# A fused two-block kernel on one core: the values of two channel tiles by seven products instead of eight

## The chip, the cores and the metric

The kernel runs on one core of a Trainium2 chip. The metric is the device time of the whole program in microseconds (us), less is better. Engines are named as the profile names them: PE (TensorE; PEld its weight loads), DVE (VectorE), ACT (ScalarE), POOL (GpSimd) and SP (SyncE, which issues most DMAs).

## The reference, cut to what matters

Two blocks, each `x = x + s * g`, on 2 batches of 512 tokens and 512 features, all float32. The first block is an autocorrelation with a small mixture of experts, the second a state-space mixer (128 heads of 64 channels in 8 groups, states of 128, chunks of 128 tokens) with a gated feed-forward layer. The change lies in the mixer, after its input's norm `h`:

```python
proj = jnp.einsum('bsd,od->bso', h, in_proj_w)
gate = proj[..., :D_INNER]
hBC = proj[..., D_INNER:D_INNER + CONV_DIM]
...
hBC = jax.nn.silu(causal_conv(hBC, conv_w, conv_b))
hid = hBC[..., :D_INNER].reshape(b, s, H_M, P_M)
...
hid_dt = hid * dt[..., None]
...
Y_diag = jnp.einsum('bcijh,bcjhp->bcihp', M, hc)
...
states = jnp.einsum('bclhn,bhcl,bclhp->bchpn', Bh, decay_states, hc)
...
yg = y * jax.nn.silu(gate)
...
out = jnp.einsum('bsd,od->bso', y, out_proj_w)
```

The values `hid` are 8192 channels: a projection of 512 features per channel, a causal convolution of four taps, a SiLU. The gate is a projection of the same size without the convolution.

## The kernel before, in words

The first part (about 600 us) computes the first block, the mixer's norm and decays, and the feed-forward layer. The rest, some 1670 us, is the mixer. Its work is cut into 16 **units** (8 groups of 16 heads, each for 2 batches), a unit into 8 **tiles** of 128 channels (two heads) by 512 tokens, and `step(d)` handles two tiles at a time. So a unit has four steps, told apart by `t` = 0, 2, 4, 6, and there are 63 steps and a tail. Each step works on several pairs of tiles at different stages:

- tiles `a` (2d, 2d+1): `products` (L1170, L1179) multiply the decay matrices and the states into `py`, and `finish_y` (L1198, L1199) makes y on DVE.
- tiles `n` (the next pair): `transposed` (L1222, PE) and `values` (L1232, DVE) bring `hid` into token order; `decays` (ACT: clamp L1246, exp into PSUM L1260; DVE: multiplication L1261); `states` (PE L1268, ACT copy L1270, DVE L1274); `starts` (POOL L1286); and the gate's projection, `Gates`.
- tiles `h` (the pair after that): `channels` projects the values (L1140: four matmuls of 512 columns per tile) and `conv` takes the taps, the first on ACT (L1146), three on DVE (L1151). `silu` (L1502) ends them.
- tiles `p` (the pair before): POOL multiplies y by the gate (L1590), ACT squares it (L1211), POOL sums the squares (L1215).
- the unit before: `Output` multiplies it by the output weights, by seven products of 256 columns per pair of token rows (L1463), each added into `acc` on DVE (L1477): five, five and four in the steps t=2, 4, 6. Step t=0 has no output but projects B and C of the next unit (`inner`), and t=4 makes `inner_products` of them.

`Gates` makes the gate of a pair of tiles by Winograd's form of Strassen's scheme: the 256 weight columns and 512 tokens are halved, the 512 features too, and the 2x2 blocks are multiplied in seven products of two 256-column matmuls (L608) instead of eight. POOL forms sums of the weight blocks ahead (`row_sums`, L582); sums of `hT` are kept in `th` for all tiles. The partial sums that several blocks share are read out between the products, by ACT copies (L1335) and DVE adds (L1339), and the last product of a half accumulates in its PSUM bank.

The order of work is written out by hand: under `manual_schedule` each engine runs its instructions in program order, and waits are placed where tiles and PSUM banks are shared. The eight PSUM banks are `pj` 2, `tr` 2, `yy` 2, `of` 1, `de` 1. Of the 63 steps, 57 take the branch `if gates:`; the others (`plain` ones in the first and last unit) project the gate directly.

Of the kernel before, what the change touches and what calls it, by code (L numbers as in the profile page):

```python
# [15 lines left out]
P = 128  # L16
# [32 lines left out]
def fused_kernel(  # L49
# [41 lines left out]
    after = const.tile([P, P], F32, tag="after", name="after")  # L91
    make_lower_triangular(nc, after, val=1.0, diag=False)
    ones = const.tile([P, P], F32, tag="ones", name="ones")
    nc.gpsimd.memset(ones, 1.0)

# [27 lines left out]
    hand = early.enter_context(tc.tile_pool(name="hand", bufs=1, side="right"))  # L123
    epsum = early.enter_context(tc.tile_pool(name="eps", bufs=1, space=PSUM))
# [926 lines left out]
    with ExitStack() as sm:  # L1051
# [92 lines left out]
        def conv(ps, ct, dst):  # L1144

            nc.scalar.activation(  # L1146
                dst, ps, AF.Identity, bias=cb[:, ct : ct + 1], scale=cw[:, ct, KCONV - 1 : KCONV]
            )
            silus.append(dst)
# [69 lines left out]
        def transposed(s):  # L1219
            px = psum.tile([P, NCH, P], F32, tag="tr", name=f"px{s}", bufs=2)  # L1220
            for c in range(NCH):
                nc.tensor.transpose(px[:, c, :], hid[s][:, bass.ts(c, P)], ident)  # L1222
            return px
# [39 lines left out]
        def states(s, hcd):  # L1263

            u, g, b, t, h0 = place(s)
            pn = psum.tile([P, NCH - 1, P], F32, tag="tr", name=f"pn{s}", bufs=2)
            for c in range(NCH - 1):
                nc.tensor.matmul(pn[:, c, :], Bss[u][:, c, :], hcd[:, c, :], start=True, stop=True)  # L1268
# [24 lines left out]
        def gate(s, bank, room="sgt"):  # L1293

            u, g, b, t, h0 = place(s)
            pg = psum.tile([P, S], F32, tag=bank, name=f"gt{s}", bufs=1 + (bank == "pj"))
            project(lambda k: wgs[s // 2][:, k, bass.ts(s % 2, P)], b, pg)
            bufs = {} if room == "sgt" else {"bufs": 4}
            sgs[s] = wk.tile([P, S], F32, tag=room, name=f"sgt{s}", **bufs)
            return sgs[s], pg  # L1300

        class Gates:
# [4 lines left out]
            def __init__(self, s):  # L1307
# [3 lines left out]
                sw = wk.tile([P, 4, 2, P], F32, tag="sw", name=f"sw{s}", bufs=1)  # L1311
                sw = [sw[:, i] for i in range(4)]
                row_sums(w, *sw)
                self.factors = seven(w, sw, hT[:, :, bass.ts(b, S)], b)

            def multiply(self, *which):
                for i in which:
                    if i == 1:
                        self.ps = psum.tile(
                            [P, 2, HD], F32, tag="pj", name=f"gt{self.s}", bufs=2  # L1320
# [27 lines left out]
        def channels(s):  # L1348
# [3 lines left out]
            ps = psum.tile([P, S], F32, tag="pj", name=f"pjh{s}", bufs=2)  # L1352
# [19 lines left out]
        def inner_products(u):  # L1372

            pb = psum.tile([P, NCH, P], F32, tag="tr", name=f"pb{u}", bufs=2)
# [122 lines left out]
        outs, ahead, rest_of_sums = {}, {}, set()  # L1497
# [7 lines left out]
        def head():  # L1505
# [30 lines left out]
            pxs = [transposed(s) for s in range(2)]  # L1536
# [6 lines left out]
            for s, x in enumerate(hcd):  # L1543
# [11 lines left out]
        def step(d):  # L1555
# [43 lines left out]

            for s, py in zip(a[:1], pys):  # L1600
                finish_y(s, py)
            for s in n[:1]:
# [5 lines left out]
            for s in n[:1]:  # L1608
                decays(s, 1)
                starts(s)  # L1610
            first = [channels(s) for s in h[:1]]
            pxs = [transposed(s) for s in n]
# [12 lines left out]
            def squares():  # L1625
                if t == 0 and went:
                    pss = psum.tile([P, NCH], F32, tag="tr", name=f"ssq{u - 1}", bufs=2)
                    for c in range(NCH):
# [3 lines left out]
                            ones[:, 0:1],  # L1632
# [10 lines left out]
            if gates:  # L1643
                if o:
                    o.multiply(1)
                if projected is not None:
                    first.append(inner(projected, 0))
                for x in first[:1]:
                    conv(*x)
                for s in n[1:]:  # L1650
                    decays(s, 0)
                    decays(s, 1)
                    starts(s)
                hcd = [values(s, px) for s, px in zip(n[:1], pxs)]
                root()
                gates.multiply(1, 5)
                second = [channels(s) for s in h[1:]]
                gates.copy(0, 0)
                gates.multiply(2, 6)
                for x in first[1:]:  # L1660
                    conv(*x)
                hcd += [values(s, px) for s, px in zip(n[1:], pxs[1:])]
                if o:
                    o.add()
                    if t == 4:
                        o.sums(1)
# [32 lines left out]
                pss = squares()  # L1699
                gates.silu()  # L1700
                silu()
                mean(pss)
                if o:
                    o.add()
            else:
# [31 lines left out]
                for s, x in zip(n, hcd):  # L1737
# [20 lines left out]
            if n and not plain(d + 1) and d + 1 < steps - 1:  # L1758
# [150 lines left out]
```

## Time and profile before

| | us |
|---|---|
| median of three runs | 2275.12 (2275.07 to 2275.14) |
| profiled execution | 2273.2 |
| its span (first to last instruction) | 2271.5 |
| granted PE clock, mean | 0.998 |
| DVE busy, ACT busy, POOL busy | 1431.9, 1243.9, 1135.3 |
| L1140 pjh (values), PE busy | 467.5 in 1024 records, mean 599 ns |
| L608 gt from th and sw (three of the gate's products), PE busy | 175.6 in 684 records (57 steps, 12 each), mean 379 ns |

The profile counts each float32 matmul as two records (`x8` is one tile's four matmuls). The mean duration of a record includes the time in which its end overlaps the next one, so the pace of PE is read from the starts of successive groups. "Idle before" gives what an engine waited for; the last column of a group names who released it.

### The profile page before, as it was taken

Reading aid. Unit: us, or ns where it says so; the run is one execution under the profiler, and the core shown is the slowest. Engines: PE = TensorE matmul, PEld = TensorE weight load, DVE = VectorE, ACT = ScalarE, POOL = GpSimd, SP = SyncE. Lnnn points to the kernel's source line nnn. Section 1 sums busy time; section 2 is a strip of 40 time slices with the busy share of each in tenths; the row PEclk is TensorE's granted clock in tenths of the full one; section 3 lists DMA queues with packets and bytes.
Section 4 is the critical chain, followed back from the end, with each engine's and each line's share of the span. In section 5 each row is a group of like instructions: output and inputs, shape, how many; then the busy total and the mean of one; then the engine's idle time right before and its main releaser. Section 6 shows DMA issues by size and latency. Waiting matters only on the chain.

```text
span 2271.5 us, 33304 instructions
## 1 busy us (share of the span) xinstructions
PE 2239.9 (99%) x11776; PEld 1589.5 (70%) x11776; DVE 1431.9 (63%) x2761; ACT 1243.9 (55%) x2693; POOL 1135.3 (50%) x996
## 2 busy tenths in 40 slices
PE   8999999999999999999999999999999999999998
PEld 4545576864567777777777777777677777777776
DVE  5273578445776766666666666666767666766653
ACT  4141323315775657566666666666656565666650
POOL 4160532232454457444755474555556455645484
PEclk9999999999999999999999999999999999999999
DMA  4021366746553435444544444454545444544442
GB/s 169 1 93 37 127 218 217 257 167 214 155 165 121 130 121 163 137 139 152 164 123 130 158 126 124 136 177 132 150 129 163 121 130 121 177 130 139 148 140 93
DMA packets 195509, 323.37 MB, mean 142 GB/s; under 512 B 17680, under 2 KB 129168, under 8 KB 192912
## 3 DMA queue, kind: packets, MB, share of 16 engines
q1 hardware_dynamic: 188944, 300.28, 43.2%
q0 software_dynamic: 6400, 20.98, 2.4%
q8 instruction: 94, 1.54, 0.3%
q14 instruction: 71, 0.58, 0.1%
HBM read 294.45 MB, written 26.74 MB: 141 GB/s over the span
## 4 chain that ended last, share of the span: by engine, by line
PE 92%; ACT 3%; DVE 2%; DMA 1%; issue 1%; POOL 0%; SPq 0%; ACTq 0%; POOLq 0%; DVEq 0%
PE pjh L1140 18%; PE of L1463 14%; PE gt L608 13%; PE py L1170 5%; PE pjbc L1140 4%; PE pf L1019 4%; PE pn L1268 4%; PE py L1179 3%; PE ofy L1463 2%; PE sh L523 2%; PE hu L362 2%; PE pg L608 2%; PE pu L608 2%; PE gty L608 2%; PE px L1222 2%; PE gt L1140 2%
## 5 line engine op out<-in xcount | busy, mean ns | idle before, releaser
L1140 PE MATMUL pjh<-hT,wh 128*128 128x512 f32 x1024 | 467.5, 599 | 0.5
L1286 POOL TENSOR_TENSOR eb<-CT,eb 128x768 f32<-128x768 f32 x128 | 230.2, 1817 | 445.0 <-DMA eb<-ea_d 408.0
L1151 DVE SCALAR_TENSOR_TENSOR hid<-pjh,cw,hid 128x511 f32<-128x511 f32 (+2 forms) x384 | 286.8, 747 | 81.9 <-ACT hid L1146 72.9
L1140 PEld LDWEIGHTS pjh<-hT,wh 128*128 128x128 f32 x1024 | 187.8, 190 | 202.5 <-issue 200.2
L1246 ACT ACTIVATE cs<-cs,sl 128x128 f32<-128x128 f32 x1024 | 323.6, 388 | 1.0 <-DMA cs<-cs_d 1.0
L582 POOL TENSOR_TENSOR sw<-wg 128x256 f32<-128x256 f32 x114 | 83.9, 736 | 287.6 <-PE gt L608 287.6
L1261 DVE TENSOR_TENSOR cs<-de,CB 128x512 f32<-128x512 f32 x256 | 175.3, 685 | 78.3 <-ACT de L1260 78.3
L1146 ACT ACTIVATE hid<-pjh,cb,cw 128x512 f32<-128x512 f32 x128 | 99.2, 775 | 166.1 <-PE pjh L1140 166.1
L1260 ACT ACTIVATE de<-cs 128x512 f32<-128x512 f32 x256 | 154.1, 602 | 49.5 <-DVE cs L1261 43.3
L1170 PE MATMUL py<-cs,hc 128*64 128x128 f32 x2048 | 180.4, 276 | 0.0
L1477 DVE SCALAR_TENSOR_TENSOR acc<-of,rg,acc 128x256 f32<-128x256 f32 x192 | 92.1, 480 | 138.3 <-PE of L1463 137.6
L608 PE MATMUL gt<-th,sw 128*128 128x256 f32 x684 | 175.6, 379 | 0.0
L1590 POOL TENSOR_TENSOR y<-y,sgt 128x512 f32<-128x512 f32 x124 | 161.7, 1325 | 12.2 <-ACT sgt L1346 10.4
L1179 PE MATMUL py<-eb,st 128*64 128x128 f32 x1536 | 149.2, 273 | 0.0
L1215 POOL TENSOR_TENSOR sums<-sums,sq 128x512 f32<-128x512 f32 x110 | 139.9, 1272 | 18.4 <-ACT sq L1211 14.7
L1274 DVE SCALAR_TENSOR_TENSOR st<-st,sl,pn 128x64 f32<-128x64 f32 x512 | 103.8, 275 | 62.9 <-ACT st L1270 62.9
L608 PEld LDWEIGHTS gt<-th,sw 128*128 128x128 f32 x684 | 126.7, 190 | 21.4 <-issue 6.7
L1170 PEld LDWEIGHTS py<-cs,hc 128*64 128x64 f32 x2048 | 121.5, 137 | 15.4 <-issue 13.4
L1199 DVE SCALAR_TENSOR_TENSOR y<-hid,Dcol,y 128x512 f32<-128x512 f32 x128 | 126.8, 990 | 4.5
L1463 PE MATMUL of<-wt,y 128*128 128x256 f32 x512 | 120.6, 379 | 0.0
L1335 ACT COPY sgt<-gt 128x256 f32<-128x256 f32 x171 | 63.4, 371 | 104.4 <-PE gt L608 104.4
L1198 DVE TENSOR_TENSOR y<-py,el 128x512 f32<-128x512 f32 x128 | 87.5, 684 | 51.7 <-PE py L1179 51.7
(337 smaller groups left out, 4511.5 us busy)
## 6 DMA issues: line engine op xcount, KB each, us to landing
cs<-cs_d SPq DMA_DIRECT2D x128, 512.0 KB, 4.3
eb<-ea_d SPq DMA_DIRECT2D x256, 192.0 KB, 6.1
wh<-in_in_wT SPq DMA_DIRECT2D x64, 512.0 KB, 9.0
wg<-in_in_wT SPq DMA_DIRECT2D x64, 512.0 KB, 7.4
el<-ea_d SPq DMA_DIRECT2D x256, 128.0 KB, 7.6
wo<-wo_d SPq DMA_DIRECT2D x16, 1024.0 KB, 8.6
wop<-in_out_wT SPq DMA_DIRECT2D x39, 256.0 KB, 3.0
wo_d<-wop POOLq DMA_DIRECT2D x39, 256.0 KB, 2.8
```

Of the source, the lines that this page charges most:

```text
L608: nc.tensor.matmul(ps, x[:, k, :], y[:, k, :], start=(first and k == 0), stop=(k == 1), skip_group_check=True,)
L1140: nc.tensor.matmul(ps, w_of(k), hT[:, k, bass.ts(b, S)], start=(k == 0), stop=(k == KD - 1))
L1151: nc.vector.scalar_tensor_tensor(dst[:, j:], ps[:, : S - j], cw[:, ct, KCONV - 1 - j : KCONV - j], dst[:, j:], ALU.mult, ALU.add,)
L1170: nc.tensor.matmul(py[bass.ts(hh, HP), bass.ts(c, P)], hc[:, c, bass.ts(hh, HP)], M[:, hh, bass.ts(c, P)], start=True, stop=(c == 0),)
L1179: nc.tensor.matmul(py[bass.ts(hh, HP), bass.ts(c, P)], st[:, c - 1, bass.ts(hh, HP)], cte[:, hh, bass.ts(c - 1, P)], start=False, stop=True,)
L1215: nc.gpsimd.tensor_tensor(sums[u], sums[u], q, ALU.add)
L1246: nc.scalar.activation(m[:, bass.ts(c, P)], m[:, bass.ts(c, P)], AF.Relu, bias=sls[g][:, 3, b * NCH + c, h0 + hh : h0 + hh + 1], scale=-1.0,)
L1260: nc.scalar.activation(pe, m, AF.Exp, scale=-1.0)
L1261: nc.vector.tensor_tensor(m, pe, CBs[s // GT].rearrange("p c i -> p (c i)"), ALU.mult)
L1286: nc.gpsimd.tensor_tensor(eb_t[s], CTs[s // GT][:, P:].unsqueeze(1).to_broadcast([P, 2, S - P]), eb_t[s], ALU.mult,)
L1463: nc.tensor.matmul(ps, x[:, k, :], y[:, k, :], start=(first and k == 0), stop=(k == 3), skip_group_check=True,)
L1590: nc.gpsimd.tensor_tensor(y_of(s), y_of(s), sgs.pop(s), ALU.mult)
```

## The change

The values of a pair of tiles `h` are now made by the same seven-product scheme as the gate, by a new class `Values`; the 512-column products remain in the plain steps. Blocks of the result are completed inside their two PSUM banks (`pj`), so that `conv` reads them there: ACT copies a partial sum to the still unused `hid` tile, and DVE adds it back to the bank. The weight sums are made by POOL at the end of the step before, and of the four sums of each scheme one now overwrites a block of the weights in place.

The order of the step is rewritten for the 57 steps: transposition, values and decays of the first tile of `n` come first, its states are begun (`begun`) before the second tile's, both decays of a tile are separated by the copies of `Values`, both convs come in the second half of the step, and each output product has its addition right behind it. One `tr` bank becomes a third `pj` bank. `conv` is split so that C's DVE taps come last in step t=0. The `ones` and `after` matrices move to the early pool, and a column of ones is taken from `upper`.

```diff
@@ -1143,9 +1142,15 @@

         def conv(ps, ct, dst):

+            first_tap(ps, ct, dst)
+            taps(ps, ct, dst)
+
+        def first_tap(ps, ct, dst):
             nc.scalar.activation(
                 dst, ps, AF.Identity, bias=cb[:, ct : ct + 1], scale=cw[:, ct, KCONV - 1 : KCONV]
             )
+
+        def taps(ps, ct, dst):
             silus.append(dst)
             for j in range(1, KCONV):
                 nc.vector.scalar_tensor_tensor(
@@ -1216,8 +1221,9 @@

             return add

-        def transposed(s):
-            px = psum.tile([P, NCH, P], F32, tag="tr", name=f"px{s}", bufs=2)
+        def transposed(s, spare=False):
+            tag, bufs = ("pj", 3) if spare else ("tr", 1)
+            px = psum.tile([P, NCH, P], F32, tag=tag, name=f"px{s}", bufs=bufs)
             for c in range(NCH):
...
@@ -1260,12 +1266,19 @@
             nc.scalar.activation(pe, m, AF.Exp, scale=-1.0)
             nc.vector.tensor_tensor(m, pe, CBs[s // GT].rearrange("p c i -> p (c i)"), ALU.mult)

-        def states(s, hcd):
+        def begun(s, hcd, spare=False):
+
+            tag, bufs = ("pj", 3) if spare else ("tr", 1)
+            pn = psum.tile([P, NCH - 1, P], F32, tag=tag, name=f"pn{s}", bufs=bufs)
+            for c in range(NCH - 1):
+                nc.tensor.matmul(
+                    pn[:, c, :], Bss[s // GT][:, c, :], hcd[:, c, :], start=True, stop=True
+                )
+            return pn
+
+        def states(s, pn):

             u, g, b, t, h0 = place(s)
-            pn = psum.tile([P, NCH - 1, P], F32, tag="tr", name=f"pn{s}", bufs=2)
-            for c in range(NCH - 1):
-                nc.tensor.matmul(pn[:, c, :], Bss[u][:, c, :], hcd[:, c, :], start=True, stop=True)
...
@@ -1293,12 +1306,64 @@
...
+        def pair_sums(w, tag, s):
+
+
+            sw = wk.tile([P, 3, 2, P], F32, tag=tag, name=f"{tag}{s}", bufs=1)
+            sw = [sw[:, 0], sw[:, 1], row_quarters(w)[2], sw[:, 2]]
+            row_sums(w, *sw)
+            return sw
+
+        class Values:
+
+
+
+            def __init__(self, s):
+                self.s = s
+                u, g, b, t, h0 = place(s)
+                self.ct = g * GT + t
+                w = whs[s // 2]
+                self.factors = seven(w, pair_sums(w, "sh", s), hT[:, :, bass.ts(b, S)], b)
+                self.ps = {}
+
+            def multiply(self, *which):
+                for i in which:
+                    tile = int(i not in (2, 3))
+                    if i in (1, 2):
+                        self.ps[tile] = psum.tile(
+                            [P, 2, HD], F32, tag="pj", name=f"pjh{self.s + tile}", bufs=3
+                        )
+                    product(self.ps[tile][:, int(i in (3, 5))], self.factors[i], i in (1, 2))
+
+            def quarter(self, i, j):
+                return hid[self.s + i][:, bass.ts(j, HD)]
+
+            def copy(self, i, j):
+
+                if (i, j) == (0, 0):
+                    for s in (self.s, self.s + 1):
+                        hid[s] = wk.tile([P, S], F32, tag="hid", name=f"hid{s}", bufs=4)
+                nc.scalar.copy(self.quarter(i, j), self.ps[1][:, 0])
+
+            def add(self, i, j):
+
+                q = self.ps[i][:, j]
+                nc.vector.tensor_tensor(q, q, self.quarter(i, j), ALU.add)
+
+            def add_fifth(self):
+                q = self.quarter(0, 1)
+                nc.vector.tensor_tensor(q, self.ps[1][:, 1], q, ALU.add)
+
+            def sum(self, i):
+                ps = self.ps[i].rearrange("p j n -> p (j n)")
+                return ps, self.ct + i, hid[self.s + i]
+
...
@@ -1308,16 +1373,13 @@
                 self.s = s
                 u, g, b, t, h0 = place(s)
                 w = wgs[s // 2]
-                sw = wk.tile([P, 4, 2, P], F32, tag="sw", name=f"sw{s}", bufs=1)
-                sw = [sw[:, i] for i in range(4)]
-                row_sums(w, *sw)
-                self.factors = seven(w, sw, hT[:, :, bass.ts(b, S)], b)
+                self.factors = seven(w, pair_sums(w, "sw", s), hT[:, :, bass.ts(b, S)], b)
...
@@ -1597,19 +1660,22 @@
             if (d - 1) in rest_of_sums:
                 sum_out(g, 2)

+            early = () if gates else n[:1]
             for s, py in zip(a[:1], pys):
                 finish_y(s, py)
-            for s in n[:1]:
+            for s in early:
                 decays(s, 0)
             for s, py in zip(a[1:], pys[1:]):
                 finish_y(s, py)
             for s in n:
                 load_rest(s)
-            for s in n[:1]:
+            for s in early:
                 decays(s, 1)
                 starts(s)
-            first = [channels(s) for s in h[:1]]
-            pxs = [transposed(s) for s in n]
+            hids = made_ahead.pop(d, None)
+            if not gates:
+                first = [channels(s) for s in h[:1]]
+                pxs = [transposed(s, s % 2) for s in n]
...
             def squares():
                 if t == 0 and went:
-                    pss = psum.tile([P, NCH], F32, tag="tr", name=f"ssq{u - 1}", bufs=2)
+                    pss = psum.tile([P, NCH], F32, tag="de", name=f"ssq{u - 1}", bufs=1)
                     for c in range(NCH):
                         nc.tensor.matmul(
                             pss[:, c : c + 1],
                             sums[u - 1][:, bass.ts(c, P)],
-                            ones[:, 0:1],
+                            upper[:, P - 1 : P],
                             start=True,
                             stop=True,
                         )
@@ -1641,67 +1707,92 @@
...
             if gates:
-                if o:
-                    o.multiply(1)
+
+                def output(n=1):
+                    if o:
+                        o.multiply(n)
+
+                def added():
+                    if o:
+                        o.add()
+
+                late = t == 2
+                px = transposed(n[0])
+                hids.multiply(1, 5)
+                hcd = [values(n[0], px)]
+                decays(n[0], 0)
+                hids.copy(0, 0)
+                hids.multiply(2, 3)
+                hids.add(0, 0)
+                decays(n[0], 1)
+                starts(n[0])
+                output()
                 if projected is not None:
-                    first.append(inner(projected, 0))
-                for x in first[:1]:
-                    conv(*x)
-                for s in n[1:]:
-                    decays(s, 0)
-                    decays(s, 1)
-                    starts(s)
-                hcd = [values(s, px) for s, px in zip(n[:1], pxs)]
+                    b_of = inner(projected, 0)
+                px = transposed(n[1])
+                hids.multiply(6)
+                if not late:
+                    added()
+                hcd.append(values(n[1], px))
+                decays(n[1], 0)
+                if projected is not None:
+                    conv(*b_of)
+                hids.copy(0, 1)
+                gates.multiply(1, 5)
+                decays(n[1], 1)
+                starts(n[1])
                 root()
-                gates.multiply(1, 5)
-                second = [channels(s) for s in h[1:]]
+                if late:
+                    added()
+                if t == 4 and o:
+                    o.sums(1)
+                hids.multiply(7)
+                hids.copy(1, 1)
                 gates.copy(0, 0)
-                gates.multiply(2, 6)
-                for x in first[1:]:
-                    conv(*x)
-                hcd += [values(s, px) for s, px in zip(n[1:], pxs[1:])]
-                if o:
-                    o.add()
-                    if t == 4:
-                        o.sums(1)
-                    o.multiply(1)
-                gates.add(0, 0)
+                gates.multiply(2)
+                pn = begun(n[0], hcd[0])
                 for f in [square(s) for s in p]:
                     f()
-                for x in second:
-                    conv(*x)
+                hids.multiply(4)
+                states(n[0], pn)
+                hids.add_fifth()
+                hids.add(0, 1)
+                hids.add(1, 1)
+                output()
+                added()
+                if projected is not None:
+                    c_of = inner(projected, 1, True)
+                    c_of(range(0, KD // 2))
+                conv(*hids.sum(0))
+                first_sums()
+                gates.multiply(6)
                 gates.copy(0, 1)
-                if o:
-                    o.add()
-                first_sums()
-                silu()
-                for s, x in zip(n, hcd):
-                    states(s, x)
-                third = None
+                gates.add(0, 0)
+                output()
+                added()
                 if projected is not None:
-                    third = inner(projected, 1, True)
-                    third(range(0, KD // 2))
+                    c_of = c_of(range(KD // 2, KD))
+                conv(*hids.sum(1))
                 gates.multiply(7)
                 gates.copy(1, 1)
                 gates.add(1, 1)
-                if third:
-                    third = third(range(KD // 2, KD))
-                if o:
-                    o.multiply(1)
+                pn = begun(n[1], hcd[1])
+                states(n[1], pn)
+                output()
+                added()
+                if projected is not None:
+                    first_tap(*c_of)
+                pss = squares()
                 gates.multiply(4, 3)
-                if o:
-                    o.add()
+                silu()
                 gates.add(0, 1)
-                if third:
-                    conv(*third)
-                if o:
-                    o.multiply(2 if t < 6 else 1)
-                pss = squares()
+                output(int(t < 6))
                 gates.silu()
-                silu()
                 mean(pss)
-                if o:
-                    o.add()
+                added()
+                if projected is not None:
+
+                    taps(*c_of)
...
             else:
...
@@ -1756,6 +1848,7 @@
             if multiplied is not None:
                 inner_products(multiplied)
             if n and not plain(d + 1) and d + 1 < steps - 1:
+                made_ahead[d + 1] = Values(2 * d + 6)
                 ahead[d + 1] = Gates(n[0])
             if t == 6 and 0 <= u < units:
```

The remaining lines adapt the head, the plain steps and the tail to the new tags (`pj` with three buffers, `tr` with one) and to `begun`, and move the two constant matrices.

More of the change, by code (lines that the diff above doesn't have):

```diff
@@ L90, in fused_kernel @@
     make_upper_triangular(nc, upper, val=1.0, diag=True)
[L91 to L94, printed above, removed]
     acc = [const.tile([P, D], F32, tag=f"acc{rt}", name=f"acc{rt}") for rt in range(NT)]
@@ L123, in fused_kernel @@
     hand = early.enter_context(tc.tile_pool(name="hand", bufs=1, side="right"))
+    after = hand.tile([P, P], F32, tag="after", name="after")
+    make_lower_triangular(nc, after, val=1.0, diag=False)
+    ones = hand.tile([P, P], F32, tag="ones", name="ones")
+    nc.gpsimd.memset(ones, 1.0)
     epsum = early.enter_context(tc.tile_pool(name="eps", bufs=1, space=PSUM))
@@ L1295, in gate @@
             u, g, b, t, h0 = place(s)
-            pg = psum.tile([P, S], F32, tag=bank, name=f"gt{s}", bufs=1 + (bank == "pj"))
+            pg = psum.tile([P, S], F32, tag=bank, name=f"gt{s}", bufs=1 + 2 * (bank == "pj"))
             project(lambda k: wgs[s // 2][:, k, bass.ts(s % 2, P)], b, pg)
@@ L1319, in multiply @@
                         self.ps = psum.tile(
-                            [P, 2, HD], F32, tag="pj", name=f"gt{self.s}", bufs=2
+                            [P, 2, HD], F32, tag="pj", name=f"gt{self.s}", bufs=3
                         )
@@ L1351, in channels @@
             hid[s] = wk.tile([P, S], F32, tag="hid", name=f"hid{s}", bufs=4)
-            ps = psum.tile([P, S], F32, tag="pj", name=f"pjh{s}", bufs=2)
+            ps = psum.tile([P, S], F32, tag="pj", name=f"pjh{s}", bufs=3)
             project(lambda k: whs[s // 2][:, k, bass.ts(s % 2, P)], b, ps)
@@ L1372, in inner_products @@
         def inner_products(u):
-            pb = psum.tile([P, NCH, P], F32, tag="tr", name=f"pb{u}", bufs=2)
+            pb = psum.tile([P, NCH, P], F32, tag="tr", name=f"pb{u}", bufs=1)
             for c in range(NCH):
@@ L1495, in final @@
             nc.sync.dma_start(out[rows(rt), cols], fx)
-        outs, ahead, rest_of_sums = {}, {}, set()
+        outs, ahead, made_ahead, rest_of_sums = {}, {}, {}, set()
         steps = tiles // 2
@@ L1535, in head @@
             first = channels(2)
-            pxs = [transposed(s) for s in range(2)]
+            pxs = [transposed(s, s == 1) for s in range(2)]
             for hh in range(2):
@@ L1542, in head @@
             held = gate(1, "of")
-            for s, x in enumerate(hcd):
+            pns = [begun(s, x, s == 1) for s, x in enumerate(hcd)]
+            for s, x in enumerate(pns):
                 states(s, x)
@@ L1736, in step @@
                     o.add()
-                for s, x in zip(n, hcd):
+                pns = [begun(s, x, s % 2) for s, x in zip(n, hcd)]
+                for s, x in zip(n, pns):
                     states(s, x)
@@ L1792, in tail @@
             e.room = lambda p: [extra[0][:, 0], extra[0][:, 1], extra[1][:, 0]]
-            e.banks = lambda p: (("of", 1), ("yy", 2)) if p == 0 else (("pj", 2), ("yy", 2))
+            e.banks = lambda p: (("of", 1), ("yy", 2)) if p == 0 else (("pj", 3), ("yy", 2))
             o.multiply(1)
@@ L1803, in tail @@
                         q[:, bass.ts(c, P)],
-                        ones[:, 0:1],
+                        upper[:, P - 1 : P],
                         start=(i == 0),
```

## The prediction

> **What bounds the kernel now.** I read the page's first and fourth parts first, then the stretches of one unit (16 heads of one batch, four steps), then the timeline of those steps.
>
> ```profile
> PE 2239.9 (99%) x11776; PEld 1589.5 (70%) x11776; DVE 1431.9 (63%) x2761; ACT 1243.9 (55%) x2693; POOL 1135.3 (50%) x996
> ...
> PE 92%; ACT 3%; DVE 2%; DMA 1%; issue 1%; POOL 0%; SPq 0%; ACTq 0%; POOLq 0%; DVEq 0%
> ```
>
> PE is busy almost always and 92% of the chain that ended last is PE. A busy PE could still hide waits, so I cut one unit at the starts of its steps (t=0, 2, 4, 6 in this order):
>
> ```profile
> 1282.50:1309.10 26.60, 26.60 (x148) 17.50 (x146) 18.58 (x34) 17.33 (x38) 15.35 (x12) 1.00 0.62 208
> 1309.10:1336.30 27.20, 27.20 (x161) 20.98 (x160) 18.63 (x37) 20.66 (x47) 23.17 (x20) 1.00 0.49 136
> 1336.30:1364.70 28.40, 28.40 (x173) 22.52 (x172) 17.81 (x36) 15.19 (x34) 17.61 (x16) 1.00 0.41 121
> 1364.70:1390.10 25.40, 25.40 (x154) 19.56 (x152) 16.57 (x33) 15.88 (x36) 8.29 (x7) 1.00 0.46 136
> ```
>
> The columns are length, PE, PEld, DVE, ACT, POOL, clock, DMA share and GB/s. PE fills every step, at full clock; DVE is busy 17 to 19 us of 25 to 28. So a step lasts as long as its matmuls, and the time falls if PE gets fewer of them and waits for nobody. DVE has room as an average; whether it has room where PE needs it is the question.
>
> **What goes.** The 57 steps of the `if gates` branch project two tiles with eight 512-column products (two records each).
>
> ```profile
> 1347.38 3.60 PE L1140 MATMUL pjh<-hT,wh 128*128 128x512 f32 x8
> 1350.81 1.03 PE L608 MATMUL gty<-hT,wg 128*128 128x256 f32 x4
> 1351.67 1.03 PE L608 MATMUL gt<-th,sw 128*128 128x256 f32 x4
> 1352.54 1.89 PE L1463 MATMUL of<-wt,y 128*128 128x256 f32 x8
> ```
>
> The second column includes the pipeline's drain, so I take starts to starts. A tile costs 1350.81-1347.38 = 3.43 us (3.53 for the first tile of a step, at 1312.30 to 1315.83), and one of the seven products 0.863 (1351.67-1350.81 = 0.86, 1352.54-1351.67 = 0.87). Eight become seven at half width: 3.53+3.43 = 6.96 against 7x0.863 = 6.04. I take 0.93 less per step. 57x0.93 = **53 us** is the most that the change can bring. The rest of PE's work is the same (`ones` becomes a column of `upper`).
>
> **What comes, off PE.** Per step: three ACT copies (L1335's form, 0.37), four DVE adds (L1339's form, 0.41), four POOL sums (L582, 0.73): 1.1, 1.6 and 2.9 us. POOL's sums for the next step wait only for their weights' DMA and for this step's early products, so they fall between the squares' adds and the gate's sums, where POOL idled 3.79 us (1329.2 to 1333.0) in the step t=2 and longer in the others; I charge nothing. Without that cover product 5 of the next step would wait up to 2.9 us. Two of the adds write a PSUM bank, which no DVE row of the mixing stage shows. The nearest rows are 0.41 (one PSUM operand, 256 columns) and 0.68 (512 columns); reading is no cheaper in either, so I exclude a gain and take 0.41; 0.68 would cost up to 0.5 us in the steps where the adds are on the path (t=0 and 2), 15 us in all. The smaller edits (third `pj` bank for the second `tr` bank, other branches) touch nothing on which PE waits in the trace; by PE's longest single wait in this stage, 1.8 us, I bound them at -1.8 to +1.8 and take 0.
>
> **Where PE will wait.** In the old order, the taps of the convs and the gate's additions were spread over the step. In the new one both convs come late, and DVE works them off in line: add of output 2, taps of tile 1, gate add (0,0), add of output 3, taps of tile 2, gate add (1,1). Product 4 of the gate must follow gate add (1,1): it writes the other half of that add's bank.
>
> ```profile
> 1305.91 0.41 DVE L1339 TENSOR_TENSOR sgt<-sgt,gt 128x256 f32<-128x256 f32 x1
> 1306.38 1.13 PE L608 MATMUL gt<-th,wg 128*128 128x256 f32 x4
> ```
>
> Here that wait shows already: the add ends 1306.32, product 4 starts 0.06 later. [...]
>
> Durations for the queue, start to start: taps 2.24 (a conv at 1372.55, the next op at 1374.79), gate add 0.34 (1380.44 to 1380.78), output add about 0.40, PE's end to DVE's start 0.20 (product 7 ends 1329.30, ACT's copy starts 1329.50), DVE to PE 0.06.
>
> - **t=4 and t=6.** From the end of output 2 on PE to gate product 4, DVE needs 0.20+0.40+2.24+0.34+0.40+2.24+0.42+0.06 = 6.30 us. PE has in between product 6 (0.86), output 3 (1.73), product 7 (0.86), one tile's states (0.67, half of the 1.34 in the chain) and output 4 (1.73) = 5.85. Wait **0.45**; gain 0.93-0.45 = 0.48 each.
> - **t=0.** No outputs, but two halves of C's projection (1.72 each) and the taps of B, which delay the second tile's decay and, through ACT's order (copies, squares 1.15, states' copy), the states. I laid the step out from its start (products 3.21, transposition 0.44, ...): ACT's states' copy ends 16.6, DVE's states and three adds 18.6, ident 19.05, taps 21.3, gate add 21.65, taps 23.9, gate add 24.3; PE is ready for product 4 at 23.6. Wait **0.75**. The old step had about 0.3 of small waits (26.6 against 26.3 of matmuls), so 0.45 is gained.
> - **t=2.** It inherits the taps of C, now the last DVE work of t=0 with no output behind them to cover: DVE is free 2.95 us into the step. The first finish of y waits for POOL as well:
>
> ```profile
> 1311.33 2.96 POOL L1590 TENSOR_TENSOR y<-y,sgt 128x512 f32<-128x512 f32 x2
> ...
> 1311.76 1.40 DVE L1199 SCALAR_TENSOR_TENSOR y<-hid,Dcol,y 128x512 f32<-128x512 f32 x1
> ...
> 1338.83 0.75 DVE L1199 SCALAR_TENSOR_TENSOR y<-hid,Dcol,y 128x512 f32<-128x512 f32 x1
> ```
>
> L1199 takes 0.75 alone and 1.40 beside POOL. So values end at 7.7, the first decay at 8.35, and ACT, whose order is decay, copy, decay, runs behind: exp 9.0, clamp 10.2, exp 10.85, copy 11.1, clamp 12.4, exp 13.0, then the square root's table load 1.28 and root 0.2, copy (1,1) 14.7. Product 4 of the values is ready at 14.25: wait **0.48**. Squares and states' copy end 16.3, states 17.1, adds 18.3, output add 18.7, taps 20.95, 0.34, 0.40, taps 23.95, gate add 24.4; product 4 of the gate is ready at 23.15: wait **1.27**. Together 1.75 against 0.93 saved: 0.8 lost.
>
> [...]
>
> **Sum.** Per unit -0.45+0.8-0.48-0.48 = -0.6; 14 whole units give -8.4, the 57th step (a t=2) +0.8: **-7.6**. From the profiled execution's 2273.2 (span 2271.5 and 1.7 around it) that is 2265.6; the median of the runs is 1.9 above the profiled one, so 2267.5, and I say **2267**.
>
> **Rivals.**
> - *The waits are covered* (DVE's queue is shorter than the starts suggest, or the late convs start earlier). For it: t=4 and t=6 lack only 0.45 us of 6.3; DVE is busy 66% only. Against it: both sums are rows of this trace. Without any wait 2275-53 = 2222; with half of mine 2245.
> - *The new order costs more than the products save.* Mechanism: ACT and DVE pass each other tiles in turn (exp, multiply, copy, product, copy) from the step's start, and product 4 of the gate sits at the end of it. It decides as soon as the mean wait in a step passes 0.93 us. If all steps wait as I have t=2 waiting, 57x(1.75-0.93) = +47: 2322; if t=4 and t=6 wait as t=0 does and t=2 another 0.7 us, 14x(-0.45+1.5-0.18-0.18) = +10, 2285. For it: ACT is at 20.66 of 27.2 us in t=2, and my layout knows only the waits that I looked for. Against it: three of four steps have their wait under the price.
> - *An even trade*: gains and waits within 0.2%. That is about what a measurement of this kernel can tell from no change (4.5 us). My sum is only 3 us beyond it.
> - *The seven products don't replace the eight*: excluded, the changed order has fourteen 256-column matmuls in place of eight of 512 in those steps.
>
> **Numbers.** My case, a small gain (2250 to 2270): 0.38. Covered waits (2222 to 2250): 0.15. Even (2271 to 2279): 0.13. Slower (2280 to 2322): 0.34. So faster 0.53, same 0.13, slower 0.34. The range leaves out the lowest of the covered case and the top of the slower one: 2236 to 2300; it takes in the PSUM adds at their upper bound (2267+15 = 2282) and the smaller edits. The likeliest sign's own range is 2236 to 2270.
>
> **What would show it.** Right: PE's idle or lengthened places sit at product 4 of the gate, released by DVE's gate add, 0.3 to 0.6 us in t=4 and t=6, more in t=2; step t=2 is longer than 27.2 us, t=4 and t=6 are shorter than 28.4 and 25.4; the new PSUM adds take about 0.41. Wrong: waits at products 6 or 7 on ACT's copies, at product 5 on POOL's sums, or at the second transposition on DVE's values in most steps (then the slower rival), or no wait at all in t=4 and t=6 (then the covered one); L1199 far above 0.99 on average.

## The result, and the profile after

The change gives 2270.16 us (2267.27 to 2272.19, 17 runs) against 2273.93 us of the kernel before (2271.16 to 2277.14, 17 runs): ratio 0.9983, 95% interval 0.9975 to 0.9990, so 3.8 us less; 2267 was forecast. The profiled execution took 2268.78 us, with a span of 2266.8 (before 2271.5), at a mean granted clock of 0.998.

The page of the kernel after, first and fourth parts:

```profile
PE 2208.6 (97%) x12460; PEld 1715.3 (76%) x12460; DVE 1524.7 (67%) x2989; ACT 1296.5 (57%) x2864; POOL 1311.1 (58%) x1224
...
PE 73%; DVE 15%; ACT 7%; issue 3%; DMA 2%; SPq 0%; POOL 0%; ACTq 0%; POOLq 0%; DVEq 0%
```

PE is busy 31 us less, but the span fell by 5 only. The chain that ended last was 92% PE; now 22% of it runs over DVE and ACT. The same unit of work cut at its steps (t=0, 2, 4, 6; columns as in the prediction):

```profile
1279.40:1305.60 26.20, 25.53 (x157) 19.72 (x156) 18.93 (x36) 18.45 (x41) 17.52 (x13) 1.00 0.65 211
1305.60:1333.30 27.70, 27.06 (x173) 23.39 (x173) 21.09 (x43) 20.66 (x48) 27.10 (x26) 1.00 0.47 134
1333.30:1361.40 28.10, 27.87 (x185) 24.61 (x184) 19.90 (x39) 17.91 (x42) 20.46 (x21) 1.00 0.40 122
1361.40:1386.50 25.10, 24.87 (x167) 21.66 (x166) 18.18 (x37) 15.73 (x36) 11.50 (x11) 1.00 0.47 137
```

PE no longer fills its steps: it is idle 0.67, 0.64, 0.23 and 0.23 us in them. Steps t=0, 4 and 6 are shorter than before, t=2 is longer. The three largest sums of PE's waits in the mixing stage (us in all, times, longest):

```profile
PE gt L607 <- DVE sgt L1401: 24.1, 57, 0.7
PE pjh L607 <- ACT hid L1352: 2.0, 9, 0.5
PE ssq L1695 <- POOL sums L1220: 1.9, 1, 1.9
```

57 times, once a step, the gate's product waits for DVE's addition. "Idle" here counts less than is lost: in t=4 it is 0.23 us and by starts 0.49. The record of the output ahead of the wait lasts 1.89 us, but without a wait the next matmul starts 1.72 after such a one (1351.07 to 1352.79), and the product that waited takes 0.97 to the next start (1356.44 to 1357.41), others 0.86. Below I go by starts and by whole steps. Steps are given as means over the units 1 to 14.

The wait in the step t=4, with DVE's queue before it (timeline):

```profile
1350.40 0.48 DVE L1539 SCALAR_TENSOR_TENSOR acc<-of,rg,acc 128x256 f32<-128x256 f32 x1 [0.25 <-PE of L1525]
1350.81 2.31 DVE L1156 SCALAR_TENSOR_TENSOR hid<-pjh,cw,hid 128x511 f32<-128x511 f32 x3
1353.03 0.41 DVE L1401 TENSOR_TENSOR sgt<-sgt,gty 128x256 f32<-128x256 f32 x1
1353.36 0.48 DVE L1539 SCALAR_TENSOR_TENSOR acc<-of,rg,acc 128x256 f32<-128x256 f32 x1
1353.76 2.31 DVE L1156 SCALAR_TENSOR_TENSOR hid<-pjh,cw,hid 128x511 f32<-128x511 f32 x3
...
1355.98 0.41 DVE L1401 TENSOR_TENSOR sgt<-sgt,gt 128x256 f32<-128x256 f32 x1
1356.44 1.13 PE L607 MATMUL gt<-th,wg 128*128 128x256 f32 x4 [0.23 <-DVE sgt L1401]
```

Output's add, taps, gate add, output's add, taps, gate add: DVE goes through them without a gap, and PE starts 0.05 us after the last one ends (1356.39). From the first add to PE's start it is 6.04 us; the forecast's durations for it came to 6.10.

In t=2 a second wait comes on top, at the values' product 4:

```profile
1318.23 1.28 ACT L1683 ACT_TABLE_LOAD   x1
1319.52 0.20 ACT L1683 ACTIVATE rg<-rg 128x4 f32<-128x4 f32 x1
1319.63 0.35 ACT L1352 COPY hid<-pjh 128x256 f32<-128x256 f32 x1
1320.04 1.13 PE L607 MATMUL pjh<-th,wh 128*128 128x256 f32 x4
```

The product (1320.04) follows a copy that stood behind the square root and its table load on ACT.

### The profile page after: what moved, and what is told of

Its sections match the earlier page's. It is cut to its first block, busy times and chain, and to the rows that moved or that the text cites. A ratio compares the mean times of both kernels' runs of the same rounds, so it can differ in the third digit from the quotient of the medians.

```text
span 2266.8 us, 35459 instructions
## 1 busy us (share of the span) xinstructions
PE 2208.6 (97%) x12460; PEld 1715.3 (76%) x12460; DVE 1524.7 (67%) x2989; ACT 1296.5 (57%) x2864; POOL 1311.1 (58%) x1224
## 4 chain that ended last, share of the span: by engine, by line
PE 73%; DVE 15%; ACT 7%; issue 3%; DMA 2%; SPq 0%; POOL 0%; ACTq 0%; POOLq 0%; DVEq 0%
PE pjh L607 12%; PE gt L607 9%; PE of L1525 8%; DVE hid L1156 7%; PE py L1175 5%; PE pjbc L1139 4%; PE pf L1018 4%; PE py L1184 3%; PE hu L361 2%; PE sh L522 2%; PE pg L607 2%; PE px L1228 2%; PE pu L607 2%; PE pn L1274 2%; DVE sgt L1401 2%
## 5 line engine op out<-in xcount | busy, mean ns | idle before, releaser
L1156 DVE SCALAR_TENSOR_TENSOR hid<-pjh,cw,hid 128x511 f32<-128x511 f32 (+2 forms) x384 | 286.6, 747 | 23.7 <-ACT hid L1149 12.7
L1653 POOL TENSOR_TENSOR y<-y,sgt 128x512 f32<-128x512 f32 x124 | 174.5, 1428 | 14.6 <-ACT sgt L1408 12.3
L1287 DVE SCALAR_TENSOR_TENSOR st<-st,sl,pn 128x64 f32<-128x64 f32 x512 | 108.6, 276 | 77.3 <-ACT st L1283 77.3
L607 PE MATMUL gt<-th,wg 128*128 128x256 f32 x456 | 123.0, 392 | 24.1 <-DVE sgt L1401 24.1
L1352 ACT COPY hid<-pjh 128x256 f32<-128x256 f32 x171 | 63.4, 370 | 145.1 <-PE pjh L607 145.1
L581 POOL TENSOR_TENSOR sw<-wg 128x256 f32<-128x256 f32 x57 | 41.6, 731 | 177.9 <-PE gt L607 177.8
L1204 DVE SCALAR_TENSOR_TENSOR y<-hid,Dcol,y 128x512 f32<-128x512 f32 x128 | 132.3, 1033 | 4.5
L607 PEld LDWEIGHTS gt<-th,wg 128*128 128x128 f32 x456 | 81.9, 189 | 57.3 <-DVE sgt L1401 42.5
L1525 PE MATMUL of<-wo,s 128*128 128x256 f32 x496 | 118.9, 383 | 2.4 <-DVE acc L1539 1.2
L607 PE MATMUL pjh<-th,wh 128*128 128x256 f32 x456 | 118.7, 383 | 2.1 <-ACT hid L1352 2.0
```

Of the source, the lines that this page charges most:

```text
L607: nc.tensor.matmul(ps, x[:, k, :], y[:, k, :], start=(first and k == 0), stop=(k == 1), skip_group_check=True,)
L1156: nc.vector.scalar_tensor_tensor(dst[:, j:], ps[:, : S - j], cw[:, ct, KCONV - 1 - j : KCONV - j], dst[:, j:], ALU.mult, ALU.add,)
L1204: nc.vector.scalar_tensor_tensor(y, hid.pop(s), Dcol[:, ct : ct + 1], y, ALU.mult, ALU.add)
L1525: nc.tensor.matmul(ps, x[:, k, :], y[:, k, :], start=(first and k == 0), stop=(k == 3), skip_group_check=True,)
L1653: nc.gpsimd.tensor_tensor(y_of(s), y_of(s), sgs.pop(s), ALU.mult)
```

## The experiments

Each is the kernel after with the change that is named; 3 and 7 combine several. The theory, that of the prediction: seven products save PE a fixed time in each step, and the new order gives most of it back, because DVE's and ACT's queues put what PE waits for behind what nobody waits for yet. The rivals: the products save less than counted, the order alone costs as much, or the price is that of the added copies and adds. Each experiment's time stands beside the kernel before, run on the same chip: 2273.06 us for the first four, 2273.90 for the others.

**1. The second conv's taps after the gate's addition (e1_taps).** ACT's first tap stays; the three taps on DVE go behind the second tile's states.

```diff
-                conv(*hids.sum(1))
+                second = hids.sum(1)
+                first_tap(*second)
...
                 added()
+                taps(*second)
```

> The DVE taps of the second tile's conv move behind the gate's add (1,1), the states of the second tile and the addition of output 4; nothing else changes. Theory A (what the products save is given back at product 4 of the gate, which queues behind two convs' taps on DVE): the waits of 0.99, 0.83, 0.49 and 0.49 us at that product in the steps t=0, 2, 4, 6 go; t=2 loses some of it again, as DVE comes out of t=0 about 0.6 us later. Steps about 25.3, 27.6, 27.6 and 24.6 us; 25 to 31 us less than the changed kernel, about 2238. Theory B (DVE has too much work between the states and the step's end, wherever the taps stand): PE waits for the taps at the next place instead, at outputs or at the next step's transposition, and the time falls by less than 5 us.

Measured 2234.47 us, ratio 0.9827 (0.9814 to 0.9841). Steps 25.42, 27.31, 27.63, 24.57 against 26.25, 27.86, 28.12, 25.06 after: 2.36 less in a unit. The place in a step t=4, timeline of this run:

```profile
1339.65 0.48 DVE L1539 SCALAR_TENSOR_TENSOR acc<-of,rg,acc 128x256 f32<-128x256 f32 x1
1340.62 0.42 DVE L1401 TENSOR_TENSOR sgt<-sgt,gt 128x256 f32<-128x256 f32 x1 [0.50 <-ACT sgt L1397]
...
1342.95 2.31 DVE L1156 SCALAR_TENSOR_TENSOR hid<-pjh,cw,hid 128x511 f32<-128x511 f32 x3
```
```profile
1340.62 1.89 PE L1525 MATMUL ofy<-wo,y 128*128 128x256 f32 x8
1342.35 1.03 PE L607 MATMUL gt<-th,wg 128*128 128x256 f32 x4
```

The gate's addition now waits for ACT and not for the taps; it ends at 1341.04, 1.3 us before PE comes to its product. Nobody waits for the later taps. So the wait at product 4 was DVE's queue, and its length was the taps. What stays in t=2, 1.0 us over experiment 3, is by starts 0.69 at the values' product 4, behind the table load, and 0.34 at the last output.

**2. The square root at the step's start (e2_root).**

```diff
+                root()
                 px = transposed(n[0])
...
                 starts(n[1])
-                root()
```

> In step t=2 the square root of the sums (an ACT table load of 1.28 us, the root 0.2 us, the reciprocal on DVE) moves from behind the last exponential to the step's start. Theory A (ACT is late for copy (1,1) because of that table load): the wait of 0.40 us at product 4 of the values goes, the one of 0.35 at output 4 too, and the one at product 4 of the gate falls from 0.83 to about 0.5: t=2 from 27.86 to about 26.8, 14 us in all. Theory B (step t=2 is late because DVE comes late out of t=0 with the taps of C and y waits for POOL): under 3 us.

Measured 2253.82 us, 0.9913 (0.9899 to 0.9926). Only t=2 changes, from 27.86 to 26.82; t=4 and t=6 are as after, 28.12 and 25.06. The wait for ACT's copy is gone: ACT's row (2.0 us in the kernel after) is no longer among PE's waits, whose first is

```profile
PE gt L607 <- DVE sgt L1401: 19.4, 57, 0.7
```

Product 4 of the gate waits 0.52 in t=2 instead of 0.83. The taps of C and POOL's part at the step's start are as before, so theory B (under 3 us) is out: with the root moved, t=2 waits about as long as t=4 and t=6 (0.49).

The same table load now falls into PE's first 3.2 us of products with y (in one such step 1408.67 to 1409.95, the products 1406.88 to 1410.09), where PE waits for nothing of ACT's.

**3. Both (e3_both).**

> Both moves. Theory A: all the waits named go, steps about 25.3, 26.4, 27.6 and 24.6 us; 45 to 50 us less than the changed kernel, about 2220, which is nearly the 53 us that the products save. Theory B of either: no more than the better of the two alone.

Measured **2220.61 us**, 0.9769 (0.9755 to 0.9782): faster than both kernels. The two savings add up: 2.36 and 1.04 in a unit apart, 3.36 together. Its unit:

```profile
1364.50:1389.90 25.40, 25.40 (x159) 19.63 (x158) 19.21 (x37) 18.12 (x41) 15.13 (x14) 1.00 0.45 135
1389.90:1416.20 26.30, 26.30 (x175) 23.32 (x174) 21.59 (x45) 20.32 (x46) 20.27 (x20) 1.00 0.54 151
1416.20:1443.80 27.60, 27.60 (x185) 24.68 (x184) 20.05 (x39) 18.40 (x44) 20.43 (x21) 1.00 0.39 124
1443.80:1468.40 24.60, 24.60 (x167) 21.75 (x166) 17.41 (x36) 15.71 (x36) 11.40 (x11) 1.00 0.48 140
```

PE fills every step again, with the same work on DVE, ACT and POOL as after. In this order the added copies, adds and sums cost PE nothing; what PE waited for in the kernel after was the place of the taps and of the root.

**4. The new order with eight products (e4_eight).** The values' calls stay where they are but issue the old 512-column products, one to a call and two in the last; the copies, adds and sums of the values' halves go.

```diff
-                    tile = int(i not in (2, 3))
...
-                    product(self.ps[tile][:, int(i in (3, 5))], self.factors[i], i in (1, 2))
+                    for tile, k in {
+                        1: [(0, 0)], 5: [(0, 1)], 2: [(0, 2)], 3: [(0, 3)],
+                        6: [(1, 0)], 7: [(1, 1)], 4: [(1, 2), (1, 3)],
+                    }[i]:
...
+                        project(lambda j: self.w[:, j, bass.ts(tile, P)], self.b, ps, [k])
```

> The changed kernel's order of work with the eight 512-column products in place of the seven (no copies to the values' tiles, no adds in their banks, no sums of the values' weights on POOL). Theory A (the wait in t=4 and t=6 comes from the new order, the convs standing late; the copies and adds count only in t=0 and t=2): PE has 0.93 us more per step, the wait of 0.49 in t=4 and t=6 stays, that of t=0 and t=2 goes: steps about 26.2, 27.2, 29.05, 26.0; the new order alone costs about 0.8 us per unit against the kernel before, 10 us in all (2283). Theory C (the order is free, the copies and adds of the seven products make the waits): the same as before within 4 us (2270 to 2277), no wait at product 4 of the gate.

Measured 2287.36 us, 1.0060 (1.0047 to 1.0074). So the new order alone makes the kernel 14 us slower. Its waits:

```profile
PE gt L607 <- DVE sgt L1401: 9.7, 43, 0.2
```

By starts these are 0.49 in t=2, 4 and 6, and none in t=0; theory A had t=2 free of it too, and so 2283. So in t=4 and t=6 the wait is the order's and not the products': seven products shorten the two steps by the full 0.82 and 0.83 (28.94 to 28.12, 25.89 to 25.06). In t=0 and t=2 they bring 0.00 and -0.25 (27.61 to 27.86): the time that PE no longer needs turns into waiting there, in t=2 with 0.25 more.

**5. The copies behind the exponentials (e5_copies).** Two copies of the values and one add go behind both decays of their tile.

```diff
                 decays(n[0], 0)
-                hids.copy(0, 0)
...
-                hids.add(0, 0)
                 decays(n[0], 1)
+                hids.copy(0, 0)
+                hids.add(0, 0)
...
-                hids.copy(0, 1)
                 gates.multiply(1, 5)
                 decays(n[1], 1)
+                hids.copy(0, 1)
```

> One part of the change undone: the copies (0,0) and (0,1) of the values' partial sums stand behind both exponentials of a tile on ACT instead of between them. Theory A (ACT's order decides when PE may go on with product 7): copy (0,1) ends about 12.4 us into t=4 and t=6, while PE is ready for product 7 at 11.9; waits of about 0.55 there, 0.5 in t=0 and 1.0 in t=2 (where 0.4 at product 4 goes); 2.2 us a unit more than the changed kernel, 30 us in all, about 2300. Rival (PE's other work covers the copies wherever they stand): within 4 us of the changed kernel.

Measured 2298.46 us, 1.0107 (1.0090 to 1.0124), 28 us over the kernel after. In a step t=2 of this run PE waits for a copy that comes behind four decays; ACT's lines, then PE's:

```profile
1440.03 1.26 ACT L1252 ACTIVATE cs<-cs,sl 128x128 f32<-128x128 f32 x4
1441.32 0.60 ACT L1266 ACTIVATE de<-cs 128x512 f32<-128x512 f32 x1
1441.86 0.37 ACT L1352 COPY hid<-pjh 128x256 f32<-128x256 f32 x1
```
```profile
1442.28 1.13 PE L607 MATMUL pjh<-th,wh 128*128 128x256 f32 x4 [1.08 <-ACT hid L1352]
```

The part of the change called "copies between the exponentials" does what it says: without it product 7 of the values waits 0.5 to 1.3 us in each step. The steps are only 0.51, 0.35, 0.58 and 0.51 longer than after, since in t=2 the new wait takes the place of others.

**6. The first tile's states late (e6_states).** The states of the first tile go right ahead of those of the second.

```diff
-                pn = begun(n[0], hcd[0])
...
-                states(n[0], pn)
...
+                pn = begun(n[0], hcd[0])
+                states(n[0], pn)
                 pn = begun(n[1], hcd[1])
```

> Another part undone: the states of the first tile of the pair stand late, right ahead of those of the second, in the same bank. Theory A: PE waits there for ACT's copy and DVE's four operations on the first tile's states (about 1.3 us), and those queue behind the taps of two convs, so product 4 of the gate comes later too; 1 to 2 us a step more than the changed kernel, 60 to 110 us in all. Rival (the early states only fill ACT and DVE at the wrong time): the same or faster, since the waits of the changed kernel in t=0 and t=2 hang on the states.

Measured 2486.94 us, 1.0935 (1.0919 to 1.0952): the direction as expected, the size far over it. `begun` has one buffer for its tiles, so the second tile's matmul waits until DVE's states have read the first's, and these now stand behind the conv's taps. PE's lines in one step t=2:

```profile
1421.39 0.83 PE L1274 MATMUL pn<-hcd,Bs 128*128 128x128 f32 x6
1425.04 1.04 PE L1274 MATMUL pn<-hcd,Bs 128*128 128x128 f32 x6 [2.81 <-DVE st L1287]
1425.87 3.48 PE L1525 MATMUL of<-wo,s 128*128 128x256 f32 x8
1429.19 1.03 PE L607 MATMUL gt<-th,wg 128*128 128x256 f32 x4
```

The wait is 3 us, and then four matmuls (eight records) take 3.48 us that elsewhere take 1.89. The granted clock (last column but two) of those stretches says why:

```profile
1421.40:1425.00 3.60, 0.82 (x7) 0.63 (x5) 3.42 (x9) 0.64 (x2) 2.27 (x4) 1.00 0.00 0
1425.80:1426.00 0.20, 0.20 (x3) 0.20 (x2) 0.00 (x0) 0.00 (x0) 0.00 (x0) 0.50 0.00 0
1426.40:1428.90 2.50, 2.50 (x8) 1.97 (x7) 0.86 (x4) 2.49 (x4) 0.00 (x0) 0.50 0.00 0
1429.30:1429.60 0.30, 0.30 (x3) 0.27 (x2) 0.21 (x1) 0.05 (x1) 0.00 (x0) 1.00 0.00 0
```

Here the wait is paid twice: once itself, and once in matmuls at half clock (0.50). That is so in t=0, 2 and 4, but not in t=6, which waits as long, keeps full clock and is 3.05 longer than in experiment 3 (27.62 to 24.57). By starts the second tile's matmul waits 2.2, 3.0, 3.0 and 3.0 us in the four steps, and the values' product 4 another 0.75 in t=2: 11.9 in a unit. The mean clock of 0.960 against 0.998 is 2x0.038x2486 = 189 us at half clock, half of them lost: an estimate of 6.7 us for each of 14 units, from the two clocks and the time. That makes 11.9+6.7 = 18.6; the unit is 18.60 longer than in experiment 3, which has none of these waits (122.53 to 103.93). Beside the kernel after it is 15.24 longer (122.53 to 107.29). So in the changed kernel "states early" is worth more than the products. The kernel before had both tiles' states late without this wait, in two `tr` banks; the experiment prices late states with the one bank that the change left.

**7. Eight products in the order of experiment 3 (e7_eight_both).** This parts the products from the order.

> The eight products in place of the seven as before, now in the order with both moves (second taps behind the gate's add, root at the start of t=2), in which PE does not wait. The difference to that order with seven products is the price of the products alone. Theory A: 0.93 us per step, 53 us, so about 2273, the same as the kernel before within 4 us. Rival (part of the gain came from the order and the matmuls differ by less): 2255 to 2265.

Measured 2266.53 us, 0.9969 (0.9958 to 0.9980). Its steps, 26.25, 27.12, 28.45, 25.39, are as full of PE as those of experiment 3:

```profile
1387.90:1414.20 26.30, 26.30 (x147) 17.41 (x146) 17.66 (x33) 17.24 (x38) 12.33 (x10) 1.00 0.43 131
1414.20:1441.30 27.10, 27.10 (x163) 21.02 (x162) 20.05 (x41) 19.49 (x43) 17.47 (x16) 1.00 0.48 146
1441.30:1469.70 28.40, 28.40 (x173) 22.40 (x172) 18.55 (x35) 17.42 (x41) 17.62 (x16) 1.00 0.41 121
1469.70:1495.10 25.40, 25.40 (x153) 19.45 (x152) 15.86 (x32) 14.78 (x33) 8.61 (x7) 1.00 0.50 135
```

Neither waits at the places in question, so their difference is the price of the products alone: 0.83, 0.81, 0.82 and 0.82 by the steps' means; in spans 2264.8-2218.1 = 46.7 us, 57 times 0.82. It is neither the 53 of theory A (2273) nor within the rival's range (to 2265), but nearer to the rival: against the kernel before, the order with both moves gains 7 us with the eight products still in it. So the 52 us that experiment 3 gains are 47 of the products and the rest of the order; that they come near the 53 forecast for the products alone is chance.

## Why the prediction was right, and where it was off

The mechanism was right: PE's saving is mostly returned as waits at product 4 of the gate, 57 times, behind DVE's queue, with t=2 longer and the other three shorter. With experiments 3 and 7 as kernels without these waits, each term can be measured (us for one step; the new waits are after less experiment 3, the old ones before less experiment 7):

| term | forecast, t=0, 2, 4, 6 | measured |
|---|---|---|
| seven products for eight | -0.93 in each | -0.83, -0.81, -0.82, -0.82 |
| waits of the new order | 0.75, 1.75, 0.45, 0.45 = 3.40 | 0.83, 1.55, 0.49, 0.49 = 3.36 |
| waits of the old order, and what else it lost | 0.3, 0, 0, 0 | 0.15, 0.23, 0.04, 0.04 |
| change of a unit | -0.61 | -0.38 |

- **The step that was mis-sized: what goes.** I took 3.53+3.43-6.04 = 0.92, about 0.93. The first tile's 0.1 more is no part of its products: it stands behind the 64-column products with y, and in the new order the transposition, now first there, takes 0.49 where the second tile's takes 0.44. Without it the rows give 2x3.43-6.04 = 0.82, which is what was measured. Over 57 steps that is 6.3 us less than forecast.
- **The waits** were right in sum (3.36 for 3.40) and at t=4 and t=6 within 0.04. At t=0 it is 0.08 more than forecast, and in t=2 0.20 less, so part of the agreement is that errors cancel. In t=2 I had two waits too long (1.27 for gate product 4, 0.83 by its start; 0.48 for the values' product 4, 0.38 by its start) and did not see a third, 0.34 at the last output, whose matmul waits for DVE's add of the output before. That t=2 has more than t=4 and t=6 I put down to DVE's late start (taps of C, POOL) and to the table load; experiment 2 takes nearly all of it away by moving the load alone. Whether the load would cost it without the late start, no run shows. That product 4 waits for the gate's addition is in the waits (57 times in the kernel after, 43 in experiment 4); whether it would with the two halves in two banks, no run shows.
- **The old order** lost 0.46 in a unit and not 0.3; half of it lay in t=2, where I had none. The 0.04 in t=4 and t=6 is no wait: it is the first tile's 0.10 less the 0.06 that the transposition costs in its place.
- **The adds that write PSUM.** I counted two in a step; there are three. The bounds were 0.41 and 0.68; the profile's row for the 171 of them (minimum, median, maximum in ns) says that the lower one was right:

```profile
L1357 DVE TENSOR_TENSOR pjh<-pjh,hid x171: 412/432/433, 643.2 to 2179.3; 128x256 f32<-128x256 f32 x171
```

- **POOL's sums** cost nothing worth naming: two waits of 0.8 us together in experiments 1 to 3, the only ones that the waits show. L1204 (before: L1199) rose from 990 to 1033 ns on average, beside a POOL that is busy 176 us longer: far from "far above". The taps and the gate's adds take what they took: 747 and 417 ns on average in both kernels (L1156 and L1401; before: L1151 and L1339).
- **Sum.** Fourteen units give -5.4. The rest of the difference in span is the start of the mixing stage (-0.75, and it differs by over 2 us among these kernels' runs), the first and the last unit (+2.3) and the work behind the last step's start (-0.9): together -4.7, against -7.6. The 57th step itself came out at +2.16 and not +0.8. Both this and the -0.9 are mostly the clock's, told below.
- **The rivals.** "The waits are covered" gave 2222 without any wait; experiment 3, where they are gone, has 2220.6, but only 47 us of that gain are the products' (experiment 7). "The new order costs more than the products save" needed a mean wait over 0.93 in a step. It is 3.36/4 = 0.84; against the right price, 0.82 and the old waits' 0.46/4 = 0.12, it missed by 0.1. Experiment 4 shows the order without the products on that side, 14 us slower. And "an even trade" is what the size comes to: 0.17% is under the 0.2% that I had named as the border, to which I gave 0.13. With 17 runs of each the gain itself is clear of nothing (0.9990 at most), but it is half of the forecast one. The median, 2270.16, lies on the border between my small gain (to 2270) and the even trade (from 2271), and the terms that I mis-sized, 0.43 in a unit for the products and 0.16 for the old order, are as large as the unit's gain of 0.38. So the sign was partly luck, which the 0.53 that I gave it says too.

## What to carry to other kernels

Work taken from the engine that bounds a kernel is worth only what its neighbours let it be: cut the trace into the stage's steps and add up, for the next place where the bound engine needs a result, the queue of the engine that gives it. Where a queue holds both, put what the bound engine waits for ahead of what is only needed later; here two moved calls turned a gain of 0.17% into one of 2.3%. To price such a change, run the new order with the old work (experiment 4), and both works in an order without waits (experiments 3 and 7): the order's loss of 14 us and the products' 47 were each clear by themselves, and the change as a whole, 3.8 us, hid them.

## What the runs showed of the hardware

**Behind some waits PE ran at half clock, and where they fell counted.** In the kernel after, at the last unit's step t=2, PE waits 1.89 us for POOL; then its next products run at half speed (granted clock last but two):

```profile
2159.22 1.05 PE L1695 MATMUL ssq<-upper,sums 128*128 128x1 f32 x8 [1.89 <-POOL sums L1220]
```
```profile
2160.70:2160.90 0.20, 0.20 (x8) 0.20 (x6) 0.00 (x0) 0.20 (x1) 0.20 (x1) 1.00 0.00 0
2161.20:2164.00 2.80, 2.80 (x30) 2.80 (x28) 1.27 (x2) 1.23 (x2) 2.72 (x3) 0.50 0.24 64
2164.70:2165.50 0.80, 0.80 (x13) 0.63 (x9) 0.28 (x1) 0.00 (x0) 0.72 (x2) 1.00 0.23 87
```

The products with y, 3.21 us in every other step, take 4.88: 1.67 of the 2.16 us by which this step grew. It came out so in this execution and in that of experiment 5, both with a wait of 1.9 us there; the kernel before waits 1.8 us at the same place and keeps its clock, as experiments 1 to 4 and 7 do with 0.6 to 1.2. The trace's record of the granted clock has two slow stretches in each of the kernels before and after, the second one behind the last matmul; their starts are 27.31 us apart before (2237.06 and 2264.37), 8 times 3.413, and 98.99 after (2161.10 and 2260.09), 29 times. In experiment 6, whose mean clock is 0.960, it has 44 slow stretches, and their starts are all whole multiples of 3.413 us apart. Of the 57 waits at the second tile's matmul, the 41 that begin between 0.9 us before and 0.5 us after a point of this raster are all followed by a slow stretch; the 16 that begin 1.6 to 1.9 us after one, those of t=6 among them, are not. So in that run the place in the raster decided, and not the length.

Behind the last step the kernel before had such a fall among its matmuls and the kernel after none: four matmuls (eight records) of the output projection run 3.29 us there from start to next start (2237.47 to 2240.76) against 1.81 (2233.43 to 2235.24), which is more than the 0.9 by which that part differs. From the last step's start to the end the three runs without a fall there (after, experiments 2 and 3) take 49.2 to 49.3 us, the six with one 50.2 to 50.4. The fall at 2237.1 in the kernel before comes behind no wait that the profile lists in the 7.6 us ahead of it, only behind 2.8 us of one-column matmuls (2234.67 to 2237.47); the kernel after has 2.6 us of them there and keeps its clock.

The record of the granted clock holds no values but 1.0 and 0.5 in the kernels before and after, and the slow stretches among their matmuls last 3.413 us (2161.1 to 2164.5 after, 2237.1 to 2240.5 before); those of experiment 6 in the views last 3.4 us in t=2 (1425.7 to 1429.1) and twice that in t=0. Ahead of the fall at 2161 there was no idle time but the wait of 1.89 us: PE was busy 2.31 of the 4.20 us up to 2160.2, and without a gap from there. What decides whether a wait of 1.8 or 1.9 us brings it is open.

**The table load cost what stood behind it.** Moving the load of 1.28 us, with the root behind it, to another place in the step took 1.04 us off it (experiment 2), and with the taps moved too PE waits nowhere in that step (experiment 3). In the rows shown above (1318.23) the load takes 1.28 us, and the next activation starts 1.29 us after the load's start.
